# Four stages in sequence: weights of the third brought in during the second, the last norm of a stage run inside the next, a folded projection in the first

## The chip, the cores and the metric

One core of a Trainium2 chip. The core has a matmul engine (TensorE, PE in the profile), a vector engine (DVE), a scalar engine for table functions and copies (ACT), a general engine (POOL) and a sequencer that here only issues transfers (SP). Each runs its own instructions in order and waits on semaphores for the others. The time is the device time of one execution in microseconds (us); several executions are timed, and one more is recorded by the hardware profiler. The matmuls named here are in float32.

## The reference

4096 tokens, 16 sequences of 256 with 128 features, pass through four parts, each a residual around a layer norm without gain:

```python
x = x + latent_attn(layernorm(x))   # the front
x = x + local_stack(layernorm(x))   # six layers, window 32, 16 heads of 64
x = x + mamba2(layernorm(x))        # chunked state-space scan
x = x + local_stack(layernorm(x))   # two layers, window 64, 8 heads of 64
```

In the front, with xn the normed input, there is a projection to 32 latent features from which keys and values come:

```python
q   = xn @ Wq + bq
lat = xn @ Wl + bl
k   = lat @ Wk + bk;  v = lat @ Wv + bv
out = softmax(q k^T * 8**-0.5) v @ Wo + bo     # 16 heads of 8
```

A layer of the two local stacks shifts half of the features by a token, projects to q, k and v, normalizes q and k to unit length, scales them, rotates them by position, attends in windows, projects back, and then runs a gated feed-forward net (341 hidden features, exact gelu) behind a layer norm with gain and bias. Mamba projects 128 features to 644, runs a causal convolution of four taps, a silu, the scan over chunks, a gated norm, and projects back.

## The kernel before, in words

Everything lies as features by tokens: 128 partitions, and 4096 tokens in 8 tiles of 512 (`TT`, `NTT = 8`), which the layers take as 32 blocks of 128 (`NBLK`). The residual x lives in device memory as `xd` between parts; the shifted, normed input of the next part is written to a tile `y` in on-chip memory by `norm_to_y`. That norm is a chain over four engines: a matmul with a centring matrix (L149), two ACT passes from the result (square, L151, and copy, L153), four narrow matmuls for the mean of squares (L157), a small DVE add (L161), a power on POOL (`rsqrt`, L116), four transposes that spread the result over the partitions (L167), and the DVE product (L180).

**The front** (`latent_attention`) is one loop over half heads, m from -12 to 130, sixteen m to a tile, with its order written by hand (`manual_schedule`: the instructions of each engine run in program order). An iteration issues the score matmuls of iteration m + 12 (`maximum`, L328, with the DVE reduction L337), the transposed scores and exponentials of m (`weigh`, L366 and L376) and the weighted sums of m - 2 (`apply`, L389 and L398), and advances a list of generators, `steps`, by one step. A generator `prepare(t)` makes tile t ready two tiles ahead: transposes, norm, then the matmuls for lat (L278, with the ACT pass L280), q, k and v, all through one PSUM bank `m`. q and k are spread over partitions by 16 small transfers each (`spread`, L291), half from SP, half from POOL. When a tile's sums are complete, `gather` (L412) collects them with 32 transfers at m % 16 == 1, 24 issued by POOL and 8 by SP, and `finish` (from m % 16 == 10) does the reciprocal (L418), the product (L419), the matmul with Wo (L422), the residual sum (L423) and the norm to `y`. The last tile's `finish` is not run in the front: it is returned as a generator `rest` and run, whole, in the layers.

**The six layers** (`Pipeline`, W = 32). `run` walks blocks i from 0 to 192 plus the lags, and in each i issues a hand-written list of steps, each for the block i minus its lag (PLAN32). The steps of one block go through `project` (L782, matmuls into pq and pk), squares, a Newton iteration for the length on POOL, rotation (L807, L819, L843, L863), transposes, scores, softmax, weighted sums and the output product (L1086), and four blocks at a time through the feed-forward net (`ff_` steps). One block costs about 17 us in the steady state. `load(l)` issues the weights of layer l on SP; `tables` (L699, L701) makes the rotation tables with its scales, `offsets` (L702 here, twelve matmuls and the DVE ops L718, L719) folds the norm's bias and gain into the feed-forward weights, and `products` (L726) multiplies Wv and Wo into `wvo`. For layers 1 and up, `turn_y` and `keep_y` do these in pieces beside the blocks of the layer before (`coming` gives the step); for layer 0 `rest_of_ready(0)` does offsets and products in one go at i = 3, and `run` does `rest`, the front's last `finish`, in one go at i = 6.

**Mamba** starts with the two later layers' `setup` (masks and constants on POOL, tables and biases on SP) and their `load(0)`, then its own weights (L1262 to L1284), nine transposes of them into `winT`, `woutT` and `initT` (L1292, L1299), then `fetch` (L1306) of x from `xd`, and a pipeline over the tiles: `project` (norm, input projection, convolution), scan, `leave` (residual sum, norm to `y`). Here the order is not by hand: a scheduler arranges the instructions of each engine. Each tile's `leave` is advanced beside the next tiles' work, the last tile's runs at the end.

**The two layers** (W = 64, PLAN64) first run `ready(0)` (tables and offsets), then the same block loop, 64 blocks.

Of the kernel before, what the change touches and what calls it, by code (L numbers as in the profile page):

```python
# [29 lines left out]
P = 128  # L30
# [158 lines left out]
def latent_attention(ctx: ExitStack, k: Stack, w, x_in, last, later):  # L189
# [11 lines left out]

    nc = k.nc
# [12 lines left out]
    wk = wp.tile([LAT, P], F32, name="wk")  # L215
    wl = wp.tile([P, LAT], F32, name="wl")
    wv = wp.tile([LAT, P], F32, name="wv")
    wo = last.tile([P, P], F32, name="wo")
    bq, bk, bo = (p.tile([P, 1], F32, name=n) for n, p in (("bq", wp), ("bk", wp), ("bo", last)))
    bl = wp.tile([LAT, 1], F32, name="bl")  # L220
    bv = wp.tile([P, P], F32, name="bv")
    for t, name in ((wl, "Wl"), (wq, "Wq"), (wk, "Wk"), (wv, "Wv"), (wo, "Wo")):
        nc.scalar.dma_start(t, w[name])
# [34 lines left out]
    def prepare(t):  # L258
# [7 lines left out]
        pool = last if t == NTT - 1 else work  # L266
        x = xs[t] = pool.tile([P, TT], F32, tag="x", bufs=1 if t == NTT - 1 else 5, name=k.name("x"))
# [9 lines left out]
        ps = bank()  # L277
        nc.tensor.matmul(ps[0:LAT], wl, xn, start=True, stop=True)  # L278
        lat = work.tile([LAT, TT], F32, tag="lat", bufs=1, name=k.name("lat"))
        nc.scalar.activation(lat, ps[0:LAT], AF.Identity, bias=bl)  # L280
        yield
# [4 lines left out]
        queues = (nc.sync, nc.gpsimd)  # L286
# [10 lines left out]
        nc.tensor.matmul(ps, wk, lat, start=True, stop=True)  # L297
# [4 lines left out]
        for c in range(4):  # L302
            nc.tensor.matmul(ps[:, bass.ts(c, P)], lat[:, bass.ts(c, P)], wv, start=True, stop=True)
# [5 lines left out]
        yield  # L309

# [89 lines left out]
    def gather(t):  # L400

        os = oss.pop(t)
        o, sums = (
            (last if t == NTT - 1 else work).tile([P, TT], F32, tag=i, bufs=1, name=k.name(i))
            for i in ("of", "sums")
        )
        for dst, first in ((sums, D), (o, 0)):
            for r in range(4):
                rows = slice(32 * r + first, 32 * r + first + D)
                for g in range(4):  # L410
                    queue = nc.sync if g == 3 or (t == NTT - 1 and g == 2) else nc.gpsimd
                    queue.dma_start(dst[rows_of(r, g)], os[rows, g])  # L412
        outs[t] = o, sums
# [14 lines left out]
    for _ in prepare(0):  # L428
        pass
    AHEAD, steps = 12, []  # L430
    with k.tc.manual_schedule():
        for m in range(-AHEAD, 8 * B + 3):
# [5 lines left out]
            if m % 16 == 10 and m > 16:  # L438
                steps.append(finish(m // 16 - 1, bank))
                next(steps[-1])  # L440
# [6 lines left out]
            if at % 4 == 1 and 2 <= at <= 8 * B + 1:  # L447
                subtract(at - 2)
            else:
                while steps and next(steps[0], True):  # L450
                    steps.pop(0)
            if 2 <= m <= 8 * B + 1:
                apply(m - 2)
            if m % 16 == 1 and m > 16:
                gather(m // 16 - 1)
# [85 lines left out]
class Pipeline:  # L541
# [62 lines left out]
    def open(self):  # L604

        self.wp = self.pool("w", 2)
        self.load(0)
# [59 lines left out]
    def ready(self, l):  # L667

        self.tables(l)
        self.rest_of_ready(l)  # L670

    def rest_of_ready(self, l):
        k, nc, L = self.k, self.nc, self.layers[l]
        pb = k.wide(self.homes["scores"], "pb")[:, 0:6]
        self.offsets(l, pb)
        self.add_offsets(l, pb)
        if self.W == 64:
            return
        for c0 in (0, 4):
            pm = k.wide(self.homes["scores"], "pm").rearrange("p (i c d) -> p i c d", i=2, d=P)  # L680
            for c in range(4):
                self.products(l, c0 + c, pm[:, :, c])
            nc.scalar.copy(
                L.wvo[:, 2 * c0 : 2 * c0 + 8].rearrange("p (c i) d -> p i c d", i=2), pm
            )
# [44 lines left out]
    def coming(self, n):  # L730

        l, step = divmod(n, NBLK)
        return l + 1, step if l + 1 < self.depth else -1

    @staticmethod
    def beside(yt):

        return yt[:, P : P + 768].rearrange("p (i d) -> p i d", i=2)[:, :, 0:P]

    def run(self, rest=None):  # L740
# [3 lines left out]
        if self.W == 64:  # L744
            self.ready(0)
        else:
            self.tables(0)
        with self.k.tc.manual_schedule():
            for i in range(last + max(lag for _, lag in self.plan)):
                if i % NBLK == 14 and i // NBLK + 1 < self.depth:  # L750
                    self.load(i // NBLK + 1)
                if i == 3 and self.W == 32:
                    self.rest_of_ready(0)
                if i == 6 and rest:
                    for _ in rest(lambda: self.k.wide(self.homes["norm"], "rest")[:, 0:TT]):
                        pass
# [152 lines left out]
    def turn_y(self, n):  # L909
# [8 lines left out]
        if 18 <= step < 26:  # L918
            self.products(l, step - 18, self.beside(yt))
        if step == 26:  # L920
            self.offsets(l, yt[:, P : P + 6])

    def keep_y(self, n):
# [3 lines left out]
        if 18 <= step < 26:  # L927
            c = 2 * (step - 18)
            self.nc.scalar.copy(self.layers[l].wvo[:, c : c + 2], self.beside(yt))
        if step == 26:  # L930
# [286 lines left out]

@with_exitstack
def mamba(ctx: ExitStack, k: Stack, w, pipe):
# [20 lines left out]
    for i in (0, 2):  # L1240
# [18 lines left out]
    n_in = w["in_proj_w"].shape[0]  # L1259
    n_full = n_in // P  # L1260
    win = once.tile([P, n_full + 1, P], F32, name="win")
    nc.sync.dma_start(  # L1262
        win[:, 0:n_full, :], w["in_proj_w"][0 : n_full * P].rearrange("(c p) d -> p c d", p=P)
    )
    nc.sync.dma_start(win[0:H, n_full, :], w["in_proj_w"][n_full * P : n_in])
    wout = once.tile([P, DI], F32, name="wout")
    nc.sync.dma_start(wout, w["out_proj_w"])
    cw = once.tile([P, NC, TAPS], F32, name="cw")
    nc.sync.dma_start(cw, w["conv_w"].rearrange("(c p) k -> p c k", p=P))
    cb = once.tile([P, NC], F32, name="cb")  # L1270
    nc.sync.dma_start(cb, w["conv_b"].rearrange("(c p) -> p c", p=P))
    nw = once.tile([P, 2], F32, name="nw")
    nc.sync.dma_start(nw, w["norm_w"].rearrange("(c p) -> p c", p=P))
    dcol = once.tile([P, 2], F32, name="dcol")
    init = once.tile([P, 2, P], F32, name="init")
    nc.gpsimd.memset(init, 0.0)
    for h in range(H):
        rows = slice(64 * (h % 2), 64 * (h % 2) + 64)
        nc.sync.dma_start(dcol[rows, h // 2 : h // 2 + 1], w["D"][h : h + 1].partition_broadcast(64))
        nc.sync.dma_start(init[rows, h // 2, rows], w["init_states"][h])  # L1280
    dt_bias = once.tile([P, H], F32, name="dt_bias")
    nc.sync.dma_start(dt_bias, w["dt_bias"].partition_broadcast(P))
    a_neg = once.tile([P, H], F32, name="a_neg")
    nc.sync.dma_start(a_neg, w["A_log"].partition_broadcast(P))  # L1284
    nc.scalar.activation(a_neg, a_neg, AF.Exp)
    nc.vector.tensor_scalar_mul(a_neg, a_neg, -1.0)

    winT = once.tile([P, n_in], F32, name="winT")
    for c in range(n_full + 1):
        n = P if c < n_full else H  # L1290
        pt = k.ps("t")
        nc.tensor.transpose(pt[:, 0:n], win[0:n, c, :], k.ident[0:n, 0:n])  # L1292
        k.evac(winT[:, c * P : c * P + n], pt[:, 0:n])
    woutT = once.tile([P, 2, P], F32, name="woutT")
    initT = once.tile([P, 2, P], F32, name="initT")
    for src, dst in ((wout.rearrange("p (c d) -> p c d", d=P), woutT), (init, initT)):
        pt = k.ps("t")
        for c in range(2):
# [299 lines left out]
```

## Time and profile before

| | us |
|---|---|
| median of 3 runs (lowest, highest) | 4891.48 (4888.69, 4897.18) |
| profiled execution: its own time | 4885.07 |
| profiled execution: its span | 4883.2 |
| front, to the first `pq` of the layers | 0 to 424 |
| six layers | 424 to 3756 |
| Mamba, from the last residual sum of the layers | 3756 to 4106 |
| last norm and start of the two layers | 4106 to 4118 |
| two layers | 4118 to 4883 |
| busy: PE, DVE, ACT, POOL (share of the span) | 94%, 69%, 56%, 68% |

The profiled execution spent 1.9 us outside its span, and is 6.4 us under the median. Idle time counts for an engine only if the engine sets the pace; here that is PE over most of the span. The profile also gives the clock granted to PE, as a share of its full speed: between 0.5 and 1.0 a matmul takes up to twice as long.

### The profile page before, as it was taken

The page shows a single profiled execution, that of the slowest core. Times are in us where ns is not written, and L with a number is a line of the kernel's source. Part 1 is how long each engine was busy: PE and PEld are TensorE (multiplying, and loading weights), DVE is VectorE, ACT ScalarE, POOL GpSimd, SP SyncE. Part 2 cuts the span into 40 slices and gives each one's busy share as a digit, 9 for nine tenths or more (in the row PEclk, how much of TensorE's full clock was granted, in tenths as well). Part 3 has the DMA queues.
Part 4 walks back from the last instruction along what each step waited for, and adds up shares of the span by engine and source line. Part 5 has one row for each costly group of instructions (what it writes and reads, how often), then busy time and mean ns, then how long its engine had stood idle before and what let it go on. Part 6 is the DMA issues. An engine that isn't in the chain of part 4 may idle for free.

```text
span 4883.2 us, 121363 instructions
## 1 busy us (share of the span) xinstructions
PE 4587.9 (94%) x50842; PEld 3063.1 (63%) x50842; DVE 3372.6 (69%) x4048; ACT 2743.4 (56%) x3417; POOL 3317.8 (68%) x3643
## 2 busy tenths in 40 slices
PE   8896799999999999999999999999996998899998
PEld 4453566666666666666666666666664665566665
DVE  4663677777777777777777777777772765788774
ACT  3553466566656666566666566665663453565654
POOL 3444677777777777777777777787783454777774
PEclk9997899999999999999999999999998898999999
DMA  1111010000100010001000010000101000111111
GB/s 35 37 29 43 14 39 17 16 16 18 39 16 16 17 39 16 16 17 39 16 16 16 17 39 16 17 17 22 26 23 41 15 12 18 53 47 43 49 56 39
DMA packets 208778, 131.54 MB, mean 27 GB/s; under 512 B 62029, under 2 KB 180153, under 8 KB 208233
## 3 DMA queue, kind: packets, MB, share of 16 engines
q1 hardware_dynamic: 196456, 118.12, 9.7%
q0 software_dynamic: 9984, 5.14, 0.6%
q8 instruction: 403, 6.60, 0.6%
q14 instruction: 143, 1.16, 0.1%
q10 hardware_dynamic: 1792, 0.51, 0.1%
HBM read 29.65 MB, written 8.39 MB: 8 GB/s over the span
## 4 chain that ended last, share of the span: by engine, by line
PE 69%; DVE 14%; POOL 7%; issue 5%; ACT 4%; SPq 0%; DMA 0%; DVEq 0%; ACTq 0%; POOLq 0%
PE py L1086 13%; PE pq L782 7%; PE hid L1143 6%; PE u L1060 6%; PE scores L973 5%; PE pk L782 5%; PE tq L872 4%; PE tp L1019 3%; DVE n L839 3%; PE fy L1177 3%; PE tk L872 2%; DVE rotq L807 2%; POOL rstd L116 1%; PE scores L955 1%; DVE t2q L819 1%
## 5 line engine op out<-in xcount | busy, mean ns | idle before, releaser
L1086 PE MATMUL py<-oT,wvo 128*128 128x256 f32 x3072 | 679.1, 379 | 1.2 <-ACT oT L1073 1.2
L1013 POOL TENSOR_TENSOR pr<-pr,rs 128x1024 f32<-128x1024 f32 x256 | 489.8, 1913 | 273.5 <-DVE rs L1008 241.4
L843 POOL TENSOR_TENSOR rotq<-rotq,t2q 128x1024 f32<-128x1024 f32 x256 | 605.0, 2363 | 37.0 <-DMA w<-in_L_ffn_W 22.2
L1086 PEld LDWEIGHTS py<-oT,wvo 128*128 128x128 f32 x3072 | 577.1, 190 | 75.1 <-ACT oT L1073 1.6
L1073 ACT COPY oT<-u 128x1024 f32<-128x1024 f32 x384 | 377.5, 1014 | 316.3 <-PE u L1060 307.6
L782 PE MATMUL pq<-wqkv,y 128*128 128x512 f32 x1024 | 495.6, 607 | 15.3 <-DVE t2q L819 5.4
L863 POOL TENSOR_TENSOR rotq<-rotq,rn 128x1024 f32<-128x1024 f32 x256 | 488.8, 1909 | 11.2
L807 DVE TENSOR_TENSOR rotq<-pq,tab 128x1024 f32<-128x1024 f32 x256 | 313.4, 1224 | 235.9 <-ACT sqq L793 150.5
L101 DVE TENSOR_TENSOR y<-y,py 64x256 f32<-64x256 f32 x256 | 107.2, 419 | 524.7 <-PE py L1086 523.0
L889 ACT COPY qT<-tq 128x1024 f32<-128x1024 f32 (+1 forms) x256 | 230.7, 901 | 410.9 <-PE tq L872 410.9
L843 POOL TENSOR_TENSOR rotk<-rotk,t2k 128x1024 f32<-128x1024 f32 x192 | 454.0, 2364 | 0.0
L1004 DVE TENSOR_REDUCE rs<-pr 128x16 f32<-128x1024 f32 (+1 forms) x256 | 312.3, 1220 | 157.7 <-ACT pr L997 152.9
L973 PEld LDWEIGHTS scores<-kT,qT 64*32 64x32 f32 (+1 forms) x26624 | 320.7, 108 | 157.9 <-issue 97.2
L793 ACT ACTIVATE sqq<-pq 128x1024 f32<-128x1024 f32 x256 | 261.8, 1023 | 263.1 <-PE pq L782 250.7
L1060 PE MATMUL u<-prT,vc 64*128 64x256 f32 x3072 | 405.5, 395 | 1.9
L973 PE MATMUL scores<-kT,qT 64*32 64x64 f32 (+2 forms) x26624 | 398.8, 225 | 3.0 <-issue 1.4
L782 PE MATMUL pk<-wqkv,y 128*128 128x512 f32 x768 | 393.3, 602 | 6.8 <-DMA wqkv<-in_L_ffn_Wqkv 6.8
L1143 PE MATMUL hid<-fxn,w 128*128 128x512 f32 (+1 forms) x768 | 388.9, 618 | 5.4 <-DVE ga L1165 2.7
L852 POOL TENSOR_SCALAR rn<-n 128x64 int32<-128x64 int32 (+1 forms) x128 | 30.3, 236 | 530.6 <-DVE n L839 530.6
L863 POOL TENSOR_TENSOR rotk<-rotk,rn 128x1024 f32<-128x1024 f32 x192 | 365.4, 1903 | 0.1
L997 ACT ACTIVATE pr<-pr 128x1024 f32<-128x1024 f32 x256 | 270.6, 1057 | 135.9 <-DVE pr L989 122.2
L984 DVE TENSOR_REDUCE nm<-scores 128x16 f32<-128x1024 f32 (+1 forms) x256 | 312.1, 1219 | 22.0 <-PE scores L973 20.6
(265 smaller groups left out, 9835.2 us busy)
## 6 DMA issues: line engine op xcount, KB each, us to landing
vc<-vt SPq DMA_DIRECT2D x1152, 32.0 KB
vc<-vt SPq DMA_DIRECT2D x64, 256.0 KB
vc<-vt SPq DMA_DIRECT2D x96, 128.0 KB
vc<-vt SPq DMA_DIRECT2D x576, 16.0 KB
xd<-x SPq DMA_DIRECT2D x24, 256.0 KB
wqkv<-in_L_ffn_Wqkv SPq DMA_DIRECT2D x12, 512.0 KB
x<-xd SPq DMA_DIRECT2D x24, 256.0 KB
wo<-in_L_ffn_Wo SPq DMA_DIRECT2D x6, 512.0 KB
```

What stands on the lines that cost most here:

```text
L782: self.nc.tensor.matmul(pq[:, 512 * int(half) : 512 * int(half) + 512], self.k.y[:, b, c0 : c0 + P], L.wqkv[:, col : col + 512], start=Tru ...
L807: self.nc.vector.tensor_mul(rot.rearrange("p (w h) e -> p w h e", w=ways), self.get(n, "p" + group).rearrange("p (w h e) -> p w h e", w=wa ...
L843: self.nc.gpsimd.tensor_add(rot, rot, self.done(n, "t2" + group))
L863: self.nc.gpsimd.tensor_mul(rot, rot, rn.unsqueeze(2).to_broadcast(list(rot.shape)))
L973: self.nc.tensor.matmul(sc[ch * W : (ch + 1) * W, par, c, first : self.KS], qT[rows, c, ch * W : (ch + 1) * W], kT[rows, c, t0 - W + first ...
L984: self.nc.vector.tensor_reduce(nm, self.get(n, "scores"), AX.X, ALU.max, negate=True)
L1004: self.nc.vector.tensor_reduce(rs, self.by_head(n), AX.X, ALU.add)
L1013: self.nc.gpsimd.tensor_mul(pr, pr, rs)
L1060: self.nc.tensor.matmul(pu[:, par, :, j, :], self.vc[n % 3][rows, ch, :], prT[rows, :, ch * W : (ch + 1) * W], start=True, stop=True,)
L1073: self.nc.scalar.copy(self.get(n - blk, "oT")[:, :, q0 : q0 + 64].rearrange("p (c i) q -> p i c q", i=2), self.done(n, "u" + half).rearran ...
L1086: self.nc.tensor.matmul(py, w[:, c, :], oT[:, c, :], start=(c == 0), stop=(c == last))
L1143: self.nc.tensor.matmul(pg[0:n, at : at + TT], L.w1[:, col : col + n], self.get(t, "fxn"), start=True, stop=True,)
```

## The change

**Front.** The latent projection is folded into the key and value weights once, at the start: `fold` computes Wl Wk, Wl Wv and the biases with four matmuls, two ACT copies and two DVE additions between two steps of `prepare(0)`. The step for lat in each `prepare` is gone; k and v come from xn. From tile 2 on, all 32 spread transfers of a tile are on SP. `gather` became a generator of eight pieces of four transfers, one piece per iteration, m % 16 from 1 to 8, all on POOL (in the last tile half of them on SP). `finish` starts at m % 16 == 11, behind the iteration's other steps. The last tile's buffers share one tile, the room, which Mamba's raw weights use later.

**Layers.** `rest_of_ready` is gone: layer 0's products are made beside blocks 1 to 4 and its offsets beside block 6 (`coming` answers for the first eight blocks). `rest` is advanced one step per i from i = 3. `load(0)` now stands behind the front's last gather in SP's order. Two hooks: `bring` at i = 64 loads Mamba's raw weights, and `turn` at i = 199, in the last feed-forward tile, transposes them.

**Mamba.** Its weights and transposes are gone from its start. The two layers' `setup`, `load(0)` and `ready(0)` are called inside it at its third half tile (the scheduler may place their instructions earlier). The norm of its last tile is returned and advanced in the two layers at i = 3 and on.

The core of the diff:

```diff
@@ front: prepare, gather, loop
-        ps = bank()
-        nc.tensor.matmul(ps[0:LAT], wl, xn, start=True, stop=True)
-        lat = work.tile([LAT, TT], F32, tag="lat", bufs=1, name=k.name("lat"))
-        nc.scalar.activation(lat, ps[0:LAT], AF.Identity, bias=bl)
-        yield
-        queues = (nc.sync, nc.gpsimd)
+        queues = (nc.sync, nc.gpsimd if t < 2 else nc.sync)
-        nc.tensor.matmul(ps, wk, lat, start=True, stop=True)
+        nc.tensor.matmul(ps, wk, xn, start=True, stop=True)
-            nc.tensor.matmul(ps[:, bass.ts(c, P)], lat[:, bass.ts(c, P)], wv, start=True, stop=True)
+            nc.tensor.matmul(ps[:, bass.ts(c, P)], xn[:, bass.ts(c, P)], wv, start=True, stop=True)
+    def fold():
+        for dst, of, bias, lhsT, rhs in (
+            (wk, wk0, None, None, None),
+            (wv, wv0, None, None, None),
+            (bk, None, bk, wk0, bl),
+            (bv, None, bv, bl.to_broadcast([LAT, P]), wv0),
+        ):
+            ps = bank()[:, 0 : dst.shape[1]]
+            if of is not None:
+                nc.tensor.matmul(ps, wlT, of, start=True, stop=True)
+                nc.scalar.copy(dst, ps)
+            else:
+                nc.tensor.matmul(ps, lhsT, rhs, start=True, stop=True)
+                nc.vector.tensor_add(dst, bias, ps)
-                    queue = nc.sync if g == 3 or (t == NTT - 1 and g == 2) else nc.gpsimd
+                    queue = nc.sync if t == NTT - 1 and g > 1 else nc.gpsimd
                     queue.dma_start(dst[rows_of(r, g)], os[rows, g])
+                yield
-    for _ in prepare(0):
-        pass
+    for i, _ in enumerate(prepare(0)):
+        if i == 1:
+            fold()
-            if m % 16 == 10 and m > 16:
-                steps.append(finish(m // 16 - 1, bank))
-                next(steps[-1])
             ...
+            if m % 16 == 11 and m > 16:
+                steps.append(finish(m // 16 - 1, bank))
+                next(steps[-1])
             if m % 16 == 1 and m > 16:
-                gather(m // 16 - 1)
+                pieces = gather(m // 16 - 1)
+            next(pieces, None)
@@ layers: coming, run, turn_y (keep_y alike)
+        if self.W == 32 and n < 8:
+            return 0, n + 40
-        if self.W == 64:
-            self.ready(0)
-        else:
+        if self.W == 32:
             self.tables(0)
-                if i == 3 and self.W == 32:
-                    self.rest_of_ready(0)
-                if i == 6 and rest:
-                    for _ in rest(lambda: self.k.wide(self.homes["norm"], "rest")[:, 0:TT]):
-                        pass
+                if i >= 3:
+                    next(rest, None)
+                if hooks and i in hooks:
+                    hooks[i]()
+        if 41 <= step < 45:
+            for c in range(2):
+                self.products(
+                    l, 2 * (step - 41) + c, self.beside(yt)[:, :, P * c : P * c + P]
+                )
-        if step == 26:
+        if step in (26, 46):
             self.offsets(l, yt[:, P : P + 6])
@@ Scan: bring (its constructor: 17 transfers on SP, a memset on POOL) and turn
+    def turn(self, wide):
+        k, nc = self.k, self.k.nc
+        pt = wide()
+        for c in range(self.full + 1):
+            n = min(P, self.n_in - c * P)
+            nc.tensor.transpose(
+                pt[:, c * P : c * P + n], self.win[0:n, c, :], k.ident[0:n, 0:n]
+            )
+        nc.scalar.copy(self.winT, pt[:, 0 : self.n_in])
+        nc.scalar.activation(self.a_neg, self.a_neg, AF.Exp)
+        nc.vector.tensor_scalar_mul(self.a_neg, self.a_neg, -1.0)
+        yield
+        pt = wide()
+        for i, (src, dst) in enumerate(((self.wout, self.woutT), (self.init, self.initT))):
+            for c in range(2):
+                cut = bass.ts(4 * i + c, P)
+                nc.tensor.transpose(pt[:, cut], src[:, c, :], k.ident)
+            nc.scalar.copy(
+                dst.rearrange("p c d -> p (c d)"), pt[:, 512 * i : 512 * i + 256]
+            )
+        yield
@@ Mamba
+        if b == 2:
+            later()
-    for _ in chain(others, leave(NTT - 1)):
+    for _ in others:
         pass
+    t = NTT - 1
+    nc.sync.dma_start(k.xd[:, bass.ts(t, TT)], xs[t])
+    return lambda bank: k.norm_to_y(t, xs[t], bank)
@@ tile_kernel
         with k.pairs():
             pipe.open()
-            pipe.run(rest)
+            pipe.load(0)
+            pipe.run(
+                rest(lambda: k.wide(pipe.homes["norm"], "rest")[:, 0:TT]),
+                {2 * NBLK: bring, 6 * NBLK + 7: turn},
+            )
-        pipe.setup()
         pipe.open()
+        def later():
+            pipe.setup()
+            pipe.load(0)
+            pipe.ready(0, lambda: k.ps("t"))
         with k.banks():
-            mamba(k, every("L1_attn_"), pipe)
+            rest = mamba(k, scan, room.tile([P, TT], F32, name="x_last"), later)
         with k.pairs():
-            pipe.run()
+            pipe.run(rest(lambda: k.wide(pipe.homes["norm"], "rest")[:, 0:TT]))
```

## The prediction

> **What bounds the kernel now.** I read the page's slices first, to see where PE is not full. One slice is 122 us; a digit is the busy share in tenths, and below it the granted clock.
>
> ```profile
> PE   8896799999999999999999999999996998899998
> PEclk9997899999999999999999999999998898999999
> ```
>
> PE is full through the six layers and near it in the last two. It falls short in the front (slices 0 to 2), where the layers begin (3 and 4), where Mamba begins (30) and inside and behind Mamba. The change touches just these places, so I asked for stretches around them: length, PE busy (instructions), then the other engines, then the granted clock.
>
> ```profile
> 130.00:230.00 100.00, 89.95 (x993) 50.73 (x986) 62.03 (x92) 56.93 (x114) 47.45 (x89) 0.97 0.17 35
> ...
> 424.00:600.00 176.00, 116.09 (x1350) 74.82 (x1351) 94.77 (x94) 57.63 (x66) 94.89 (x95) 0.79 0.11 26
> ...
> 700.00:3600.00 2900.00, 2860.40 (x35197) 1954.55 (x35196) 2113.86 (x2222) 1764.86 (x1981) 2184.84 (x2119) 1.00 0.09 21
> ...
> 3740.00:3785.00 45.00, 17.03 (x33) 6.85 (x34) 7.37 (x15) 5.60 (x13) 10.41 (x21) 0.58 0.31 75
> ...
> 4106.00:4118.00 12.00, 7.77 (x27) 5.74 (x28) 2.14 (x7) 1.07 (x2) 1.01 (x1) 0.50 0.06 22
> ```
>
> The long middle (PE 98.6% busy, full clock) cannot give anything: the change alters no instruction there but the hook at block 64. Everything is in the seams, and each is priced from its own rows.
>
> **The front.** PE's waits between 30 and 430 us (total, times, longest):
>
> ```profile
> PE m L167 <- POOL rstd L116: 14.7, 11, 3.3
> PE s L328 <- DVE nm L337: 8.4, 6, 1.6
> ```
>
> The first is a queue on POOL: the power stands behind the transfers of `gather`.
>
> ```profile
> 209.16 6.12 POOL L412 DMA_DIRECT2D of<-os  x12
> 215.29 1.04 POOL L116 TENSOR_TENSOR rstd<-var,neg_half 128x4 f32<-128x4 f32 x1
> ```
>
> PE's L167 then came 3.26 us late. Five such waits (2.05, 2.05, 3.26, 2.05, 2.05) make 11.5. With four transfers an iteration (4 x 0.51 = 2.1 us in an iteration of about 2.7) the power waits for one piece at most; I take all 11.5, and 5 as the poorer end.
> - The lat step: seven pairs of matmuls L278 in the loop, 1.03 us a pair where warm, are 7.2, and I add 0.13 a tile for the hop of the one bank `m`: 8.1 off a PE that is 90% busy; 4 if the waits on DVE grow by half of it.
> - `prepare(0)` loses 1.91 + 0.68 + a hop, 2.7; `fold` puts four cold matmul-and-copy hops of about 1.05 in, 4.2: +1.5. It lies before the first score, at 34.28, on the path.
> - The clock fell to half five times before 420 (two of 6.8, three of 3.4 us), two of them beside the waits above: half a clock over 23.8 us costs 12, of which I take 4; ends 0 and 9.
> - The spread on SP: 32 x 0.67 = 21.4 us per tile of about 41. q comes at m = 7, the tile is needed 13 iterations (34 us) later; 21.4 + 2 for landing leaves about 10 us. Cost 0, covered by that margin. `gather` ends at m = 8 and `finish` starts at 11, so the reciprocal (3.34 on DVE) finds its sums.
> Front: 1.5 - 8.1 - 11.5 - 4 = -22 (ends -30, with all 14.7 of the waits and 9 of the clock, and -8).
> The Trainium skill, "DMA: Bandwidth & Descriptors", section "Issuing engines are not separate DMA queues", says that issuing from several engines saves only the issuing time, usually small beside the transfer; by that rule moving transfers between SP and POOL is worth nothing, and the sum would be 11.5 us longer. The row above has the issuing time alone holding POOL for 6.12 us, so I go by the row.
>
> **Front to layers.** First pq at 424.4 after the first half of wqkv (SP issued it at 420.50, second behind one gather transfer). Now both halves stand behind all 16, at about 432, and pq near 435 to 438.7. What followed was later anyway: squares waited for `of` until 433.21, the scales were ready at 439.41 and the tables at 441.05. Late next are those tables, by 0 to 3: +1.5.
>
> **Layers, blocks 0 to 8.** DVE, then PE, at i = 6, where `rest` ran whole:
>
> ```profile
> 542.97 3.34 DVE L418 RECIPROCAL sums<-sums 128x512 f32<-128x512 f32 x1
> ```
>
> ```profile
> 547.62 2.08 PE L422 MATMUL rest<-of,wo 128*128 128x512 f32 x2 [5.82 <-DVE of L419]
> ...
> 557.02 1.12 PE L167 MATMUL rest<-ident,rstd 128*128 128x128 f32 x4 [1.37 <-POOL rstd L116]
> 557.93 2.86 PE L782 MATMUL pq<-wqkv,y 128*128 128x512 f32 x4
> ```
>
> PE did nothing but the steps of `rest` from 541.8 to 557.9: 16.1 us. At i = 3 offsets and products held back pq by 11.7 (the invert on DVE that the block needed was ready). Of these 27.8 comes back as steps between blocks: reciprocal and product on DVE ahead of the invert 4.6, Wo 2.1, centring 1.1, mean 1.5, offsets 1.8, spread 0.9, products 0.6, together 12.6. -15; ends -24 (the added steps fall into PE's idle time) and -6 (the chain by DVE and POOL takes most of it back; DVE is 54% busy here).
>
> **Hooks.** `bring`: 17 transfers x 0.4 to 0.6 = 8 us of an SP that is idle there, one POOL memset of some 1 us; PE is covered: +0.5 (0 to 2; 8 if SP held a weight load). `turn` lies ahead of the last feed-forward matmuls with nothing beside it: ten transposes (six of L1292 took 2.30 cold, four of L1299 1.59), one copy between them (bank `o` serves twice): +2.8 (2 to 6). It adds an exp, and a gelu after it, each with a table load. ACT at Mamba's start:
>
> ```profile
> 3782.48 0.37 ACT L113 COPY initT<-t 128x256 f32<-128x256 f32 x1 [3.23 <-PE t L1299]
> 3782.86 1.28 ACT L1285 ACT_TABLE_LOAD   x1
> ```
>
> A load is 1.28 us and nothing is lost before it; two are 2.6, half beside the first matmuls of the tile (in the 2.8).
> The Trainium skill, "ScalarE: Activation LUTs", section "What ACT_TABLE_LOAD costs", has about 2.66 us for a switch, a drain of 1.38 included; by it `turn` would cost some 2.8 more. The row shows no drain (copy ends 3782.85, load starts 3782.86), and I go by it.
>
> **Layers to Mamba.** SP first, then PE:
>
> ```profile
> 3757.15 2.16 SPq L617 DMA_DIRECT2D rt<-in_rope  x4
> ...
> 3781.38 1.85 SPq L1306 DMA_DIRECT2D x<-xd  x4
> ```
>
> ```profile
> 3784.74 2.04 PE L149 MATMUL t<-x,center 128*128 128x512 f32 x2 [2.30 <-DMA x<-xd]
> ```
>
> Mamba's first norm waits for x, which stands behind 44 other transfers. With the weights gone, the scheduler's order puts x behind wqkv, xd and rt alone, at 3759.4; + 3.3 as now gives 3762.7, with slack 3763.2: -21.5 (ends -23, -17). What moves behind x (scales, w1 and the rest) is needed 10 us later.
> Inside Mamba: twelve offset matmuls (2.41 cold at its end, 1.2 warm) and DVE's L699, L701, L718, L719 move in beside a PE that is 91% busy: +1.5 (ends -3 and +6, for another arrangement by the scheduler).
>
> **Mamba to the two layers.**
>
> ```profile
> 4106.40 2.08 PE L149 MATMUL t<-x,center 128*128 128x512 f32 x2 [0.51 <-DVE x L1489]
> ...
> 4117.56 2.06 PE L782 MATMUL pq<-wqkv,y 128*128 128x512 f32 x2
> ```
>
> Norm and offsets, 11.2 us with PE waiting on each hop, come off the path, as block 0 needs neither: -11 (ends -12, -8). The norm's steps in i = 3 to 5 cost +1.5 (0.5 to 3).
>
> **Sum:** -22 + 1.5 - 15 + 0.5 + 2.8 - 21.5 + 1.5 - 11 + 1.5 = -61.7. From the profiled run's 4885.07 that is 4823.4; it stood 6.4 below the median, so 4830. All good ends together: -30 + 0 - 24 + 0 + 2 - 23 - 3 - 12 + 0.5 = -89.5 (4802); all poor ends: -8 + 3 - 6 + 2 + 6 - 17 + 6 - 8 + 3 = -19 (4872).
>
> **Rivals.**
> - *Only the seams around Mamba pay.* The front is held by its DVE reductions (the wait of 8.4 above grows as PE gets shorter) and the early blocks by DVE and POOL, so both give nothing: 1.5 + 1.5 + 0.5 + 2.8 - 21.5 + 1.5 - 11 + 1.5 = -23: 4868; with half of the front and early gains 4850. For it: DVE 62% busy at 130 to 230, and chains of five engines at 424 to 600. Against: PE at 90%, and PE idle whole through `rest`.
> - *The clock comes back too.* It is 0.79 over 424 to 600, 37 us of half speed in 176; without the 16 us pause much of it stays full: early -24, front -30: 4830 - 9 - 8 = 4813.
> - *Slower: SP cannot deliver the spread.* If one spread transfer takes SP 1.34 instead of 0.67, 32 take 42.9 us, 11 beyond the margin of the tile; six tiles cost 66. With the front's gains gone with it, -40 + 66 gives 4917. It decides from 6.6 us a tile past the margin, (23.4 + 10 + 6.6 - 2) / 32 = 1.2 us per transfer; SP's issues here take 0.37 to 0.81.
> - *It doesn't do what it says:* x is fetched late still, as memory freed by the six layers or SP's order holds it: 21.5 less: 4852.
>
> **How the numbers follow.** Forecast 4830 with 0.62 (own range 4812 to 4848); only the seams, with its half case, 0.17; clock too 0.10; x late 0.06; slower 0.05. The range 4808 to 4860 leaves out the slower case, the far end of "only the seams" and a little below. What a measurement can tell from no change is about 0.2%, 10 us. Within 0.2%: only the seams pay and x is late too (-23 + 21.5), 0.03; slower: its one case, 0.05; faster: the rest, 0.92.
>
> **What would show it.** Front: the wait of L167 on rstd under 4 us, first pq near 414 instead of 424. Blocks: no PE gap over 5 us before L422; pq of block 8 some 35 us earlier than 590. Mamba: L149 within 8 us of the last residual sum (now 28.9). End: pq 1 to 3 us after the last residual sum (now 11.6). Wrong it would be by a new wait of s on ka or qa in the front, or by one on the scales (`sc`) in Mamba's DVE queue.

## The result, and the profile after

| us | before | after |
|---|---|---|
| median (lowest, highest; 4 runs each) | 4890.08 (4881.88, 4897.18) | 4844.93 (4838.34, 4845.24) |
| ratio, 95% interval | | 0.9906 (0.9893, 0.9919) |
| profiled execution: span | 4883.2 | 4843.3 |

Faster by 45 us, where 62 were forecast. All but one of the terms came out near their size; the front gave nothing. The two traces stand 40 us apart and not 45, as the profiled execution of the kernel before lay 5.0 us under its median, and that of the changed kernel on it. The table takes both profiled executions at the same marks (starts of PE's `pq` by block, of the last copy of the front's sums, L415 after and L398 before, and of the residual sums):

| stretch | forecast | measured |
|---|---|---|
| start to the front's last copy of sums (420.5, now 428.8) | -22 | +8.3 |
| from there to `pq` of block 8 (169.5, now 149.9) | +1.5 - 15 | -19.6 |
| blocks 8 to 190 | +0.5 | -1.9 |
| from there to the last residual sum (`turn`) | +2.8 | +3.0 |
| to Mamba's first matmul (28.9, now 8.4) | -21.5 | -20.4 |
| inside Mamba (321.2, now 324.8) | +1.5 | +3.6 |
| to the first `pq` of the two layers (11.6, now 0.6) | -11 | -11.1 |
| two layers | +1.5 | -1.9 |
| sum | -61.7 | -40.0 |

First the slices of the page after: PE and the clock.

```profile
PE   7986899999999999999999999999998898999998
PEclk9998999999999999999999999999999898999999
```

Slices 0 to 2 are no fuller than they were, slice 30 is. At Mamba's start, PE's first matmul still waits for x, but SP issues x at 3750.84, right behind `rt`:

```profile
3750.84 1.29 SPq L1351 DMA_DIRECT2D x<-xd  x3
```

```profile
3754.10 2.05 PE L149 MATMUL t<-x,center 128*128 128x512 f32 x2 [8.51 <-DMA x<-xd]
```

At Mamba's end, `pq` follows the last residual sum with no norm between:

```profile
4076.82 2.08 PE L1533 MATMUL o<-y,woutT 128*128 128x256 f32 x4 [0.64 <-DVE y L1530]
4079.50 3.56 PE L792 MATMUL pq<-wqkv,y 128*128 128x512 f32 x4 [0.61 <-DVE x_last L1534]
```

Where the layers begin, the stretch from the front's last copy of sums to block 8, before and after (length, PE, weight loads, DVE, ACT, POOL, then the granted clock):

```profile
420.50:590.04 169.54, 107.10 (x1184) 69.31 (x1185) 86.27 (x85) 51.90 (x60) 86.54 (x94) 0.78 0.12 31
```

```profile
428.80:578.72 149.92, 99.45 (x1185) 64.82 (x1186) 87.26 (x85) 52.24 (x62) 85.16 (x90) 0.83 0.14 34
```

Of the 19.6 us, 12.0 are PE's idle time (62.4, now 50.5). The other 7.7 are its busy time, for the same number of matmuls: it ran 75.1 us of the stretch at half clock before, and 51.2 now.

Now the front: PE's waits between 34 and 412 us, after the change (total, times, longest). `s` are the scores and `nm` their maxima, `st` the transposed scores and `pT` their exponentials, `of` the gathered sums of a tile; L442 is the matmul with Wo (L422 before).

```profile
PE m L442 <- DVE of L439: 18.4, 6, 3.4
PE st L383 <- ACT pT L393: 11.3, 14, 3.2
PE s L345 <- DMA ka<-k: 5.5, 1, 5.5
PE m L368 <- DVE y L180: 5.1, 6, 0.9
PE s L345 <- DVE nm L354: 2.5, 3, 0.9
```

The wait of 14.7 for the power on POOL, which the prediction wanted gone, is gone. In its place stands one of 18.4 that was not there: Wo's matmul for the reciprocal and the product of `finish`. One tile of it, DVE first, then PE:

```profile
242.44 3.34 DVE L438 RECIPROCAL sums<-sums 128x512 f32<-128x512 f32 x1
245.81 0.69 DVE L439 TENSOR_TENSOR of<-of,sums 128x512 f32<-128x512 f32 x1
```

```profile
246.56 2.08 PE L442 MATMUL m<-of,room 128*128 128x512 f32 x2 [3.36 <-DVE of L439]
```

`finish` now starts behind the other steps of m % 16 == 11, and its next step, Wo, comes with the first score matmuls of the following iteration only: some 1.1 us of PE work lie over 4 us of DVE work. The second wait has grown from 4.2 to 11.3; in the kernel before it was:

```profile
PE st L366 <- ACT pT L376: 4.2, 12, 0.7
```

It is ACT's: the exponentials stood behind the small transfer of the maxima (L371), and that behind a spread transfer of SP.

```profile
103.54 0.56 ACT L370 COPY nmT<-m 4x512 f32<-4x512 f32 x1
106.30 0.56 ACTq L371 DMA_DIRECT2D qa<-nmT  x1
106.90 0.37 ACT L415 COPY os<-o 128x256 f32<-128x256 f32 x1 [2.80 <-DMA qa<-q]
```

In the instruction records, ACT waits ahead of that transfer on the completion semaphore that the transfer itself will raise. SP's and ACT's transfers share eight of them in turn (31 to 34 of SP's transfers and 4 to 7 of ACT's on each, up to 420 us), and POOL's have eight others. So a transfer of ACT can find the one before it on its semaphore still standing in SP's queue, and the change put 32 spread transfers a tile there instead of 16.

The latent step is gone, but PE is not less busy for it. Before, the k matmuls took in the 32 rows of lat, and matmuls of the transposed scores ran beside them; now they take in the 128 rows of xn and run alone. Before, and then in the fastest kernel of the experiments:

```profile
180.58 0.59 PE L297 MATMUL m<-lat,wk 32*128 32x512 f32 x1
180.59 0.59 PE L366 MATMUL st<-qa,ka 32*128 32x256 f32 x2
```

```profile
225.31 1.13 PE L298 MATMUL m<-xn,wk 128*128 128x512 f32 x2
```

In a tile at full clock PE is busy for 39.5 us in both (168.18 to 212.12 us before, 209.06 to 250.93 there), with two matmuls fewer.

### The profile page after: what moved, and what is told of

It reads as the page before. It is cut to its first block, busy times and chain, and to the rows that moved or that the text cites. A ratio compares the mean times of both kernels' runs of the same rounds, so it can differ in the third digit from the quotient of the medians.

```text
span 4843.3 us, 121149 instructions
## 1 busy us (share of the span) xinstructions
PE 4570.3 (94%) x50834; PEld 3051.0 (63%) x50834; DVE 3371.2 (70%) x4050; ACT 2745.0 (57%) x3412; POOL 3297.2 (68%) x3603
## 4 chain that ended last, share of the span: by engine, by line
PE 71%; DVE 16%; POOL 5%; ACT 4%; issue 2%; SPq 1%; DMA 0%; DVEq 0%; ACTq 0%; POOLq 0%
PE py L1107 13%; PE pq L792 7%; PE hid L1164 6%; PE u L1081 6%; PE pk L792 5%; PE scores L994 5%; PE tq L882 4%; DVE n L849 3%; PE tp L1040 3%; PE fy L1198 3%; PE tk L882 2%; DVE rotq L817 2%; PE st L383 2%; POOL rstd L116 1%; DVE rotk L817 1%
```

## The experiments

Theories: A, the wait of Wo on the reciprocal ate the front's gain; B, the front is held by DVE, so a wait removed from PE comes back as another; C, the transfers of the maxima wait for SP's spread through the shared semaphores. Each kernel is the changed one with the edit shown; medians are of 4 runs where nothing else is said, beside the kernel before on the same chip (4889 to 4893).

**The old front.** The front's work as before, with layers and Mamba as changed: latent step, gather in one go, finish at 10, both queues.

```diff
-            if m % 16 == 11 and m > 16:
+            if m % 16 == 10 and m > 16:
-        queues = (nc.sync, nc.gpsimd if t < 2 else nc.sync)
+        queues = (nc.sync, nc.gpsimd)
-                    queue = nc.sync if t == NTT - 1 and g > 1 else nc.gpsimd
+                    queue = nc.sync if g == 3 or (t == NTT - 1 and g == 2) else nc.gpsimd
...
```

> The changed kernel with the front's whole work of before (latent step, gather in one go at m % 16 == 1 with 24 transfers on POOL and 8 on SP, finish at 10, spread on both queues); layers and Mamba as changed. If the new front as it stands loses (its last copy of sums came 8.3 us later than before, 428.8 against 420.5): 4837 (4833 to 4842), that is faster than the changed kernel. If the front had gained the 22 us of the prediction and something in the layers had eaten them: 4867.

4840.15 us (4837.71 to 4847.10), ratio 0.9903 (0.9878, 0.9927). The new front as it stands is worth nothing against the old; the 45 to 50 us are the layers' and Mamba's. In this run's trace the old front's last copy of sums starts at 428.5, 8 us later than in the trace of the kernel before (41.0 us at half clock up to there, against 23.9). So the +8.3 of the table is within the scatter of one trace; that the 22 us did not come is not.

**Start of finish as before**, the three lines at the head of the iteration, ahead of the score matmuls.

```diff
-            if m % 16 == 11 and m > 16:
-                steps.append(finish(m // 16 - 1, bank))
-                next(steps[-1])
...
+            if m % 16 == 10 and m > 16:
+                steps.append(finish(m // 16 - 1, bank))
+                next(steps[-1])
```

> The changed kernel with finish started at m % 16 == 10 ahead of the iteration's other steps, as in the kernel before; everything else of the new front stays. Theory A (the new wait of Wo on the reciprocal, 18.4 us over six tiles, with the half clock behind each, ate the front's gain): the wait of L442's matmul on DVE falls from 18.4 to under 4 us in all, the front ends some 20 us earlier, and the time is 4825 (4817 to 4832). Rival B (the front is held by its DVE reductions, so any time won on PE comes back as a wait of the scores on nm): that wait rises from 2.5 to 10 us or more and the time stays above 4837.

4839.26 us (4834.37 to 4842.84), ratio 0.9902 (0.9880, 0.9923). Wo's wait did not go. Without the latent step `prepare` is done an iteration sooner, so the list `steps` was empty at m = 10 and Wo slid into the same iteration:

```profile
236.62 1.43 PE L442 MATMUL m<-of,room 128*128 128x512 f32 x2 [2.87 <-ACT pT L393]
```

The releaser named here is ACT's exponential, which had long been done; DVE's product (235.82, 0.69 long) ended 0.11 before. So the run did not test theory A.

**The spread on both queues**, alone and with the edit above.

```diff
-        queues = (nc.sync, nc.gpsimd if t < 2 else nc.sync)
+        queues = (nc.sync, nc.gpsimd)
```

> The changed kernel with the spread of q and k half on SP and half on POOL in all tiles, as before. Theory C (ACT's small transfer of the maxima waits for a spread transfer that still stands in SP's queue, which holds up the exponentials: waits of 1.9 to 3.1 us at 106, 117, 148 and 207 us): ACT's waits ahead of that transfer fall from 12.6 to about 6.5 us, PE's wait of the transposed scores on pT from 11.3 to about 4, and the time falls by 6, to 4839 (4835 to 4842). Rival D (the wait is for the data of q and k itself, and POOL's eight spread transfers a step hold up the power again): L167's wait on rstd returns with 5 us or more and the time is 4845 or above.

> Both edits of the two runs beside it. Theories A and C: the two add up, 4819 (4810 to 4828). If the front is held by DVE (B), the two together give less than 8 us: above 4837.

4858.02 us (4852.29 to 4861.33), ratio 0.9940 (0.9918, 0.9961), and 4873.92 us (10 runs, 4866.03 to 4880.72), ratio 0.9973 (0.9962, 0.9984). Theory C's part came (PE's wait on pT fell from 11.3 to 5.9 and 3.6), and both were slower all the same, in a way that no theory had: POOL now had 16 spread transfers beside 32 of the gather, the gather came late, and with it the reciprocal. DVE's waits for `of`, in the second kernel:

```profile
DVE of L439 <- DMA of<-os: 32.3, 5, 8.5
```

Wo's wait rose to 27.6 and 46.5. That the power would be held up again (rival D) was wrong: PE's wait for it did not return. The move of the spread to SP and the gather's eight pieces belong together.

**Two iterations between reciprocal and Wo.** The edit of the start, and an empty step.

```diff
         nc.vector.tensor_mul(o, o, sums)
         yield
+        if t < NTT - 1:
+            yield
```

> The changed kernel with the reciprocal at the head of m % 16 == 10 and one empty step behind it, so that Wo's matmul stands behind the score and sum matmuls of m = 10 and 11 (in the run that only moved the start, Wo slid into the same iteration and each of its waits stayed at 2.9 us). Theory A: the six waits of Wo's matmul, 18.4 us, fall to under 4, the steps of 10.2 us that they make fall to about 6, and the front ends 20 us earlier up to its tail: 4825 (4817 to 4833). If the tail's gather then comes late, as in that run (POOL's last transfers of tile 6 behind each other, 10 us), 4833. Rival B (DVE holds the front): the scores' wait on nm rises to 8 us or more and the time stays above 4837.

With it, and the last but one tile's gather half on SP:

```diff
-                    queue = nc.sync if t == NTT - 1 and g > 1 else nc.gpsimd
+                    queue = nc.sync if t >= NTT - 2 and g > 1 else nc.gpsimd
```

> The run beside it, and the last but one tile's gather half on SP, which has no spread left by then, instead of all on POOL. If the gather of tile 6 holds the tail (its last transfer landed at 414.6 in the changed kernel and DVE's product waited 7.0 us for it), DVE's waits there (4.6 and 7.0 us) halve and the time is 5 to 8 below that of the run beside it. If PE had other work over those waits: no difference, within 3.

And the maxima's transfers from POOL:

```diff
-        nc.scalar.dma_start(qa[t % 3][D::32, :, c0 + blk * P : ...], nmT)
+        nc.gpsimd.dma_start(qa[t % 3][D::32, :, c0 + blk * P : ...], nmT)
```

> The run beside it with ACT's small transfers of the maxima issued by POOL instead. Theory C (those transfers wait for a completion semaphore that SP's spread transfers use too, so ACT stands until SP has issued them): ACT's waits there, 12.6 us in all, go to 0, PE's wait of the transposed scores on pT falls by 5, and the time is 5 to 8 below the run beside it. Rival E (the wait only moves to POOL, behind the gather's pieces, and the maxima come late for the transposed scores): no gain, or some us more.

4853.45 us (0.9925; 0.9911, 0.9940), 4841.79 us (0.9899; 0.9882, 0.9915) and 4846.64 us (0.9915; 0.9900, 0.9930). The gather's half on SP is worth 12, as the tail waited for POOL: DVE's waits there fell from 4.7 and 7.1 to 2.5 and 3.3, and 10.9 us lie between the two traces at the front's last copy of sums. Wo's 18.4 us went in all three, to 1.1 at most, and the time didn't: another wait took the place each time. PE's waits of the second kernel and then of the third, same stretch:

```profile
PE st L383 <- ACT pT L393: 17.5, 20, 2.3
PE s L345 <- DMA ka<-k: 5.5, 1, 5.5
PE s L345 <- DVE nm L354: 5.0, 7, 2.0
```

```profile
PE s L345 <- DVE nm L354: 22.0, 9, 6.7
PE st L383 <- ACT pT L393: 7.1, 19, 0.7
```

With the maxima on ACT, PE's next wait is for exponentials behind ACT's wait for SP (1.9 us a tile); with them on POOL, the scores wait 2.0 us a tile for the maxima, which stand behind the reciprocal on DVE. (6.7 of the 22.0 is one wait at 91 us, where POOL was making the layers' masks ahead of DVE's work on them; the third kernel is 8.5 us behind the next one at the ninth copy of sums, so about that much of its time is the first tile's maxima on POOL.) Theory A alone falls, and B is right about the reciprocal: its 4 us in one piece, product included, held up something at each place where it was tried.

**The reciprocal in halves.** With the gather's half on SP, and the maxima on POOL from tile 1 on:

```diff
-        nc.vector.reciprocal(sums, sums)
+        nc.vector.reciprocal(sums[:, 0:S], sums[:, 0:S])
+        if t < NTT - 1:
+            yield
+        nc.vector.reciprocal(sums[:, S:TT], sums[:, S:TT])
         nc.vector.tensor_mul(o, o, sums)
         yield
```

> The changed kernel with four edits of the front: the reciprocal in two halves of 256 columns (1.7 us each by the row of 3.34 for 512), one at the end of m % 16 == 11 and one a step later with the product, Wo's matmul at m % 16 == 14; the maxima's small transfers from tile 1 on issued by POOL; the last but one tile's gather half on SP. Theory F (the piece that nothing hides is the reciprocal's 3.34 us with its product on DVE: where Wo no longer waits for it, the next scores' maxima do, 2.0 us a tile, and each wait brings one stretch of 3.4 us at half clock): with halves PE's waits on DVE fall under 5 us in all, the half-clock stretch per tile goes, a tile falls from 44.3 to about 41, and the time is 4822 (4814 to 4832). Rival G (PE's own work of some 41 us per tile is the bound, so only the waits' 2 us a tile can go, and another hand-over takes their place): 4837 or above.

And the halves alone, the maxima on ACT:

> The changed kernel with the reciprocal in two halves alone (one at the end of m % 16 == 11, one with the product a step later, Wo's matmul at 14); the maxima's transfers stay on ACT and the gather as changed. If the reciprocal in one piece was the whole hand-over (theory F): Wo's 18.4 us of waits go, ACT's waits ahead of the maxima's transfers stay near 1 us a tile, and the time is within 6 of the run with four edits: 4825 (4819 to 4832). If the shared completion semaphore (theory C) is an equal part: 4834 or above, with pT's waits at 15 us or more.

4822.01 us (4818.83 to 4825.79), ratio 0.9857 (0.9840, 0.9873); the halves alone 4846.30 us (4838.24 to 4850.75), ratio 0.9907 (0.9879, 0.9936). In the halves alone Wo's wait is gone, and the scores' wait on nm is 4.2 us in all, but ACT stands still for SP:

```profile
293.67 0.56 ACT L370 COPY nmT<-m 4x512 f32<-4x512 f32 x1
298.69 0.55 ACTq L371 DMA_DIRECT2D qa<-nmT  x1
299.28 0.37 ACT L415 COPY os<-o 128x256 f32<-128x256 f32 x1 [5.05 <-DMA ka<-k]
```

ACT's time between that copy and the issue of the transfer is 25.0 us in all there, 12.6 in the changed kernel, 6.5 before, and 0.1 with POOL issuing. So neither edit does it alone: the reciprocal in one piece with the maxima on POOL gave 4846.6, halves with the maxima on ACT 4846.3, both together 4822.0. (The reciprocal in one piece also stood elsewhere, at the head of m % 16 == 10, so its place and its halving are not told apart; in one piece at 11 with the maxima on POOL was not run.) The halves alone also lack the gather's half on SP, but that moves transfers of the last tile but one alone: ahead of them, at the forty-ninth of the 64 copies of sums, they already stand 21.2 of their 22.6 us behind (357.6 against 336.4). Why ACT's time grew from 12.6 to 25.0 with the halves alone is open.

**The last gather by groups of heads.** On top of the four edits:

```diff
+        if t == NTT - 1:
+            for g in range(4):
+                for dst, first in ((sums, D), (o, 0)):
+                    for r in range(4):
+                        rows = slice(32 * r + first, 32 * r + first + D)
+                        queue = nc.sync if g % 2 else nc.gpsimd
+                        queue.dma_start(dst[rows_of(r, g)], os[rows, g])
+                yield
+            return
```

> The four edits that gave 4822, and the last tile's gather ordered by the groups of heads, the even ones on POOL and the odd ones on SP, so that SP has 8 transfers and not 16 left behind the last copy of sums (11.4 us of SP before, ahead of the layers' first weights, for which PE waits 14.1 us). If that wait is on the path: it falls by 5 to 6, the first pq comes that much earlier, and the time is 4817 (4812 to 4821). If the scales and tables behind it are late next: within 2 of 4822.

4817.44 us (4815.97 to 4818.85), ratio 0.9850 (0.9828, 0.9872): the fastest, 27 us below the changed kernel. The first `pq` moved from 416.7 to 405.1, and the next waits took more than half of it back (5.2 us for the rotation in block 1): at block 8 it leads by 4.7. The clock is whole from 83 to 390 us. One tile in three kernels, before, changed, and this one, in the columns of the prediction's stretches: length, PE, weight loads, DVE, ACT, POOL, then the granted clock:

```profile
287.90:331.90 44.00, 39.59 (x452) 22.72 (x456) 28.54 (x42) 25.70 (x52) 22.56 (x42) 1.00 0.16 33
```

```profile
288.30:333.10 44.80, 40.32 (x450) 23.30 (x454) 28.69 (x43) 25.56 (x52) 18.45 (x34) 0.96 0.15 32
```

```profile
271.50:313.40 41.90, 39.63 (x450) 22.99 (x454) 28.56 (x44) 25.29 (x51) 20.95 (x38) 1.00 0.17 34
```

The tile of the changed kernel is 2.9 us longer than that of the last: 2.2 of it PE's idle time (4.5 against 2.3), the other 0.7 its busy time at the lower clock.

**The layers' start as before.** Offsets and products at i = 3, `rest` whole at i = 6.

```diff
-                if i >= 3:
-                    next(rest, None)
+                if i == 3 and self.W == 32:
+                    self.rest_of_ready(0)
+                if self.W == 64 and i >= 3:
+                    next(rest, None)
+                if self.W == 32 and i == 6:
+                    for _ in rest:
+                        pass
```

> The changed kernel with the layers' start of before: layer 0's offsets and products in one go at i = 3, the front's last finish in one go at i = 6; loading order, front and Mamba as changed. The prediction's term for spreading these out was -15, and between the front's last copy of sums and block 8 the traces stand 19.6 apart: 4862 (4856 to 4867). If the early blocks are held by DVE and POOL anyway, under 4850.

4866.17 us (4860.20 to 4873.34), ratio 0.9953 (0.9937, 0.9969). From the front's last copy to block 8 its trace has 168.5 us, the changed kernel's 149.9, the kernel before 169.5. The hole is back:

```profile
562.72 2.07 PE L442 MATMUL rest<-room 128*128 128x512 f32 x2 [5.84 <-DVE room L439]
...
573.02 2.43 PE L808 MATMUL pq<-wqkv,y 128*128 128x512 f32 x3
```

In the changed kernel, the same matmul of `rest` slips in ahead of a `pq` and waits for nothing:

```profile
508.74 1.92 PE L442 MATMUL rest<-room 128*128 128x512 f32 x2
510.45 2.86 PE L792 MATMUL pq<-wqkv,y 128*128 128x512 f32 x4
```

**Mamba's last norm at Mamba's end again.**

```diff
-    t = NTT - 1
-    nc.sync.dma_start(k.xd[:, bass.ts(t, TT)], xs[t])
-    return lambda bank: k.norm_to_y(t, xs[t], bank)
+    for _ in leave(NTT - 1):
+        pass
+    return lambda bank: iter(())
```

> The changed kernel with the norm of Mamba's last tile run at Mamba's end again, and not in the two layers. The prediction's terms for this move were -11 + 1.5 with 2.4 of the 11 for the offsets, which stay moved here: so +7 to +9, 4853 (4850 to 4856). If that norm had gone into a wait elsewhere in the two layers: 4845, no difference.

4859.48 us (4853.64 to 4862.32), ratio 0.9934 (0.9919, 0.9949). The norm is on the path again, from 4080.55 to `pq`:

```profile
4080.55 2.07 PE L149 MATMUL t<-x_last,center 128*128 128x512 f32 x2 [0.51 <-DVE x_last L1534]
...
4089.32 3.75 PE L792 MATMUL pq<-wqkv,y 128*128 128x512 f32 x4 [1.64 <-DVE y L180]
```

The profiled execution accounts for 8.6 us (spans 4851.9 against 4843.3), as expected; the median lies 14.6 above, and the other 6 are not explained by the one trace.

## Why the prediction was right and where it was wrong

The total lay in the stated range, partly by luck: the front's miss of 30 us by the table alone leads to 4860, the range's end. The layers' start (6 better), the two layers (3), the middle (2) and the medians' 5 beyond the traces made up for half of it.

- **The middle, and the seams around Mamba: right.** SP's order decided Mamba's start (read from the two traces; no run undoes it) and the norm its end (undone above), with these terms within 2.4 us each; the two layers came out 3.4 better than forecast, for a reason that no run looked into. The Trainium skill's 2.66 us for a switch of tables ("ScalarE: Activation LUTs", section "What ACT_TABLE_LOAD costs") does not show here: `turn` cost 3.0 in all, and its two loads 1.28 each, the first of them right behind a copy (3731.01 and 0.69 long, load at 3731.72). The forecast of 2.8 had counted one copy between the banks; the second of PE's waits (1.09 us) had exp and its load in it as well, inside the range. `bring` issued 16 transfers, not 17.
- **Front to layers and early blocks: right in kind, 6 too small.** -13.5 forecast, -19.6 measured; with `rest`, offsets and products put back, 18.5 us return in the trace and 21 in the median. PE's idle time alone fell by 12.0, close to the forecast; what the sum left out are 7.7 us of busy time, the clock's, which the prediction had only as a rival.
- **The front: wrong by 30 in the table, 8 of it within the scatter of one trace.** Two terms were right: the power's wait went (14.7 to 0.3), and `fold` cost 1.6 (first score 34.28, now 35.87; 1.5 forecast). The latent step's -8.1 was not there: a pair of matmuls of 0.98 us a tile went, but PE's busy time at full clock stayed at 39.5 us a tile, as k and v over 128 rows took longer, and the prediction charged nothing for that. The step that cost the rest is the one that was put at nothing: "Cost 0, covered by that margin. `gather` ends at m = 8 and `finish` starts at 11, so the reciprocal (3.34 on DVE) finds its sums." It asked whether the reciprocal had its input, and not who waits for its output. It asked whether the spread reached its reader in time, and not who else must pass SP. Both had a new waiter: Wo (18.4), and ACT's transfers of the maxima through the shared semaphores (pT's wait from 4.2 to 11.3, with 2.2, 2.0 and 3.2 us at 108, 118 and 150 us). The front stood 6 us behind at the ninth of its 64 copies of sums, `fold` included, and 6.9 at the forty-ninth. The clock came out the other way too: no 4 us back, but 30.7 us at half clock ahead of the last copy of sums against 23.9, with one stretch of 3.4 us or more in nearly every tile, mostly at Wo's wait. None of the signs of being wrong that the prediction named came up; the first `pq`, forecast near 414, came at 442.8.
- **Which queue issues:** the Trainium skill ("DMA: Bandwidth & Descriptors", section "Issuing engines are not separate DMA queues") has only the issuing time saved by it. Moving transfers between queues did matter, but by the order behind which others stand, on both queues: 14.7 us of PE's waits went on POOL and some 7 came on SP, and the time rose by 13 when POOL got the spread as well (by 29 with the earlier start of `finish`).
- **The rivals.** "Only the seams around Mamba pay" was half right: the front gave nothing, but the wait that held it was not its DVE reductions (8.4 to 2.5 us), and the early blocks paid in full. "The clock comes back too" was right for the early blocks (7.7 us of the 9 that it priced) and wrong for the front. The slower rival did not come: SP delivered the spread in time, and no score matmul waited for ka or qa past the first. Most of the gain that was forecast was there to be had, from waits and the clock and not from the latent step: with the reciprocal halved, the maxima moved and half of a gather on SP, the front ended 18 us before that of the kernel before (402.7 against 420.5), with 6.8 us at half clock, and the time was 4822, 68 below.

## What to carry to other kernels

For each instruction that is moved, ask three things: when its input is there, how much work its reader's engine has between the two, and what stands behind it on its own engine. A long instruction on an engine that is idle a third of the time (3.3 us here, in iterations of 2.7) cost something at each place where it was tried, until it was cut into pieces. When a step is folded into others, price what the others become: here k and v over 128 rows cost PE as much as the step that they replaced had. Where waits are replaced one by one and the time stays, the cure may take two edits at once, so try them together before either is dropped.

## What was not expected of the hardware

- Transfers issued by ACT and by SP share eight completion semaphores in this program, so an engine that issues a transfer can wait for an unrelated one in the other's queue: 0.4 to 5.8 us each time, and 0.1 in all once POOL issued them.
- Waits of PE of 1.9 to 3.4 us in a tile whose PE is else some 90% busy went, more often than not, with a stretch of 3.4 or 6.8 us at half the clock (201.8, 246.2, 293.9, 338.3 and 379.3 us in the changed kernel; not behind the waits at 107.8 and 118.1). With no wait over 0.9 us the clock stayed whole for 307 us in the fastest kernel; the one with four edits, also without such a wait, still had two stretches (176.3 and 261.7). By the half clock alone, a stretch of 3.4 us costs an estimated 1.7 us, half of its length.
- A matmul over 32 rows (k before, 0.59 us) ran with matmuls of the transposed scores that started 0.01 us and 0.23 us behind it; the pair of k matmuls over 128 rows ran alone, and the next matmul started 1.06 us after the first of the pair (225.31 and 226.37).
